# Output products of an attention kernel as two row-tiled products of 64 channels, added when they are evicted

## The chip, the cores and the metric

The kernel runs on one core of a Trainium2 chip. The metric is the device time of the whole kernel in microseconds (us). A core has TensorE (matrix products, written to PSUM), VectorE, ScalarE (activations, evictions), GpSimd and SyncE (which here only issues DMA transfers). In the profile they are called PE, DVE, ACT, POOL and SP; PEld is TensorE's loading of weights, which overlaps its products. [...]

## The reference

Two layers of attention over images of 32 x 32 positions with 768 channels, four images, all fp32. Both have the same form; the second has biases on its projections and a scale that is applied twice. Cut to what matters:

```python
for layer in (0, 1):
    h = group_norm(x)                                  # 32 groups of 24 channels
    q, k, v = split(h @ Wqkv)                          # 12 heads of 64 channels
    bias = rel_h(q)[..., :, None] + rel_w(q)[..., None, :]
    attn = softmax(scale * q @ k.T + bias)             # 1024 x 1024 per head
    x = x + (attn @ v) @ Wproj + bproj
```

## The kernel before, in words

Everything is channel-major: a tile has channels on its 128 partitions and positions along its free axis. An image and layer count as one "image", `im` 0 to 7 (layer 0's four, then layer 1's four). The twelve heads go in six pairs of two heads, `pair` 0 to 5, and a pair's 1024 queries in eight blocks of 128, `n` 0 to 7. A unit is one (pair, n). The main loop runs over all 8 x 6 x 8 units in an order written out by hand; every engine takes its instructions in the order in which the loop issues them.

In each unit:

- `biases` adds the two relative-position terms on GpSimd for the unit two ahead (L319).
- `scores` for the next unit: products q k on TensorE (tile `s`, L333; a head has 64 channels, so the products of two heads are row-tiled: each uses one half of the array's rows). Two passes on VectorE take the sum with the bias and its extreme (L342, shown as CUSTOM_DVE), ScalarE takes the exponential.
- `turn` transposes the unit's weights in blocks of 32 x 32 on VectorE (tile `tb`, L370). After every second unit the tile is written to DRAM (`td`, L373) and read back in another layout (`pt`, L381). A quarter of the queries is two units. All these transfers are issued by SyncE.
- `divide` takes a reciprocal on VectorE (L353) behind the transposes, and GpSimd multiplies the next unit's weights by it (L356).
- A share of a list `todo` of other products fills TensorE: the projections of the next pair (`pj` L214, `pv` L249, 36 steps), then output products (`o` L475, 12 steps). In most pairs these shares are 6, 6, 0, 6, 12, 6, 0, 12 steps in units 0 to 7, so all of a pair's output products, four groups of three, fall into unit 7. In that unit `first` is 3: one group comes in front of the transposes, three behind them.
- At n = 6 `weigh` multiplies v with the transposed weights of quarters 0 and 1 (tile `av`, L399; column-tiled by 64), at n = 2 of the next pair those of quarters 2 and 3.

An output group takes 128 output channels by 512 positions and half of the input channels (part `p` 0 in pairs 3 to 5, part 1 in pairs 0 to 2 of the next image; the last image has three parts). It is three products of 128 channels into one PSUM bank. VectorE then adds it to what was there: to the residual and the bias (`scalar_tensor_tensor`, L486) for part 0, to the partial sum (`tensor_tensor`, L488) for part 1. For layer 0's part 1 statistics of the sum follow (L152, L154). The result is stored by SyncE (L493), issued at the start of the next unit, ahead of the read back of quarter 3.

In pair 4 the next image's six chunks are normalised on VectorE (`apply`, L193): chunks 0 to 2 in earlier units, 3 to 5 in unit 7 between the groups. `pj` of the next unit reads them.

PSUM tiles of TensorE's products other than `s` come from one pool `ps_m` with two buffers of two banks; `s` has two such tiles of its own. `pj` and `pv` are already in the form that the change gives to `o`: two row-tiled products of 64 channels into two banks, the first evicted by ScalarE and the second added by VectorE. In the last image there is no next pair; its last pair (and its tail) is filled with output products alone, whose weights `wo` are fetched by SyncE four groups ahead.

Of the kernel before, what the change touches and what calls it, by code (L numbers as in the profile page):

```python
# [31 lines left out]
FP = mybir.dt.float32  # L32
AF = mybir.ActivationFunctionType
ALU = mybir.AluOpType
ENGINES = {getattr(mybir.EngineType, e) for e in ("PE", "DVE", "Activation", "Pool", "SP")}

P = 128
B, HW, C = 4, 32, 768
S = HW * HW
NH, D = 12, 64  # L40
NC = C // P
NT = S // P
# [3 lines left out]
HALF = 512  # L46
LAYERS = 2
NP = NH // 2
# [6 lines left out]
def attention_blocks(ctx: ExitStack, tc: tile.TileContext, a: dict, out: bass.AP):  # L55
    nc = tc.nc
# [19 lines left out]
    ps_m = ctx.enter_context(tc.tile_pool(name="ps_m", bufs=2, space=PSUM))  # L76
# [9 lines left out]
    xn_of, w_of, wo_of = {im: [] for im in range(NI)}, {}, {}  # L86
# [31 lines left out]
    for l in range(LAYERS):  # L118
        tab = const.tile([P, 2, 2 * HW], FP, tag=f"tab{l}", name=f"tab{l}")
        nc.gpsimd.memset(tab, 0.0)  # L120
        for i, ax in enumerate("hw"):
            src = a[f"rel{ax}{l}"]
            n = src.shape[1]
# [9 lines left out]
    bo = []  # L133
    for l in range(LAYERS):
        t = const.tile([P, NC], FP, tag=f"bo{l}", name=f"bo{l}")
# [11 lines left out]
    def stats(im, c, i, x):  # L147

        if i == 0:
            half_stats[im] = small.tile([P, 2, 6], FP, tag="st", name=f"st_{im}_{c}")  # L150
        st = half_stats[im]
        nc.vector.bn_stats(st[:, i, :], x)  # L152
        if i == 1:
            nc.vector.bn_aggr(mv_of[im][:, c, :], st.rearrange("p i s -> p (i s)"))  # L154
# [155 lines left out]
    sc_of, st_of, tb_of, pt_of, attn_of = {}, {}, {}, {}, {}  # L310
# [40 lines left out]
    def divide(g, n):  # L351
        st = st_of[g, n]
        nc.vector.reciprocal(st[:, 2, :], st[:, 1, :])  # L353
        for h in range(2):
            sc = sc_of[g, n, h].rearrange("p k j -> p (k j)")
            nc.gpsimd.tensor_scalar(sc, sc, st[:, 2, h : h + 1], 1.0, ALU.mult, ALU.mult)  # L356
# [59 lines left out]
    def cuts(im):  # L416
        return [0, NC // 2, NC] if im + 1 < NI else [0, NC // 2, NC - 1, NC]
# [49 lines left out]
    def project_out(im, p, o, i):  # L467
        l, b = images[im]
        end = im + 1 == NI
        rows = slice(o * P, (o + 1) * P)  # L470
        cols = slice(i * HALF, (i + 1) * HALF)
        c0, c1 = cuts(im)[p : p + 2]
        t = ps_m.tile([P, S], FP, tag="m", name=f"o_{im}_{p}_{o}_{i}")[:, :HALF]
        for c in range(c0, c1):
            nc.tensor.matmul(  # L475
                t, lhsT=wo_of[im, o, c], rhs=attn_of[im * NP + c][:, cols],
                start=(c == c0), stop=(c == c1 - 1),
            )
            if c < c1 - 1:
                yield True  # L480
        if end and (p, i) == (0, 0):
            sum_of[o] = xpool.tile([P, S], FP, tag="xn", name=f"sum_{o}")
        to = sum_of[o][:, cols] if end else res_of[im, p, o, i]
        if p == 0:
            res = res_of[im, p, o, i]
            nc.vector.scalar_tensor_tensor(to, t, bo[l][:, o : o + 1], res, ALU.add, ALU.add)  # L486
        else:
            nc.vector.tensor_tensor(to, t, to, ALU.add)  # L488
        if p == 1 and l + 1 < LAYERS:
            stats(im + B, o, i, to)  # L490
        dst = (part_of[im] if p == 0 and not end else dsts[l][b])[rows, cols]
        if not end:
            early.append(lambda: nc.sync.dma_start(out=dst, in_=to))  # L493
        elif p == 2:
            nc.sync.dma_start(out=dst, in_=to)
        if i == 1 and (im, p, o, i) in place:
            if end:
                fetch(place[im, p, o, i] + 4)
            else:
                later.append(lambda: fetch(place[im, p, o, i] + 4))  # L500
        yield True
# [7 lines left out]
    def run(todo):  # L509
        while todo:  # L510
            todo.pop(0)()

    def prepare(g):

        todo = [(project_in(g, which, i), NC) for which in range(2) for i in range(2) if g < NPAIR]
        if g % 2:
            return todo + [(project_values(g - 1, i), NC) for i in (2, 3)]
        return todo + [(project_values(g, i), NC) for i in (0, 1) if g < NPAIR]
# [5 lines left out]
    def take(groups, n):  # L524

        while groups and n > 0:
            group, count = groups[0]
            if next(group, None) is None:
                groups.pop(0)
            else:  # L530
                groups[0] = (group, count - 1)
                n -= 1
        while groups and groups[0][1] == 0:
            for _ in groups.pop(0)[0]:
                pass
# [6 lines left out]
    with tc.manual_schedule(engines=ENGINES):  # L542
        for c in range(NC):
            for i in range(2):
                stats(0, c, i, xn_of[0][c][:, i * HALF : (i + 1) * HALF])
        stages, apply = norm(0)
        for n in sorted(stages):
            stages[n]()
        for c in range(NC):
            apply(c)  # L550
        todo = prepare(0)
        take(todo, 2 * NC)
        mid.pop(0)()
        take(todo, NC)
        mid.pop(0)()
        later.pop()()
        take(todo, 2 * NC)
        run(later)
        fetch(3)
        biases(0, 0)  # L560
        scores(0, 0)
        divide(0, 0)
        biases(0, 1)

        units = [(g, n) for g in range(NPAIR) for n in range(NT)]
        for at, (g, n) in enumerate(units):
            im, pair = divmod(g, NP)
            end = im + 1 == NI
            if n == 0:
                shares = [6, 6, 0, 6, 12, 6, 0, 12]  # L570
                ins = (todo if at == 0 else []) + prepare(g + 1)
                if pair < 3:
                    if at == 0:
                        shares = [12, 6, 0, 6, 12, 6, 0, 0]
                    todo = ins + (put_out(im - 1, 1, range(4 * pair, 4 * pair + 4)) if im else [])
                elif pair < NP - 1:
                    todo = ins + put_out(im, 0, range(4 * pair - 12, 4 * pair - 8))
                    if pair == 3 and not end:
                        stages, apply = norm(im + 1)
                else:  # L580
                    todo = ins + put_out(im, 0, range(8, 12))
                    if end:
                        fetch_last()
                        todo += put_out(im, 1, range(12)) + put_out(im, 2, range(0, 12, 2))
                        shares = [6, 6, 0, 6, 6, 2, 0, 4]
            if (pair, n) in loads and not end:
                load_x(im + 1, loads[pair, n])
            if im + 1 < B:
                if (pair, n) in loads0:
                    load_x(im + 1, loads0[pair, n], loads0[pair, n] + AHEAD)  # L590
                if pair < 3 and n in (1, 3, 5, 6):
                    c, i = divmod(4 * pair + n // 2, 2)
                    x = xn_of[im + 1][c % AHEAD][:, i * HALF : (i + 1) * HALF]
                    later.append(lambda c=c, i=i, x=x: stats(im + 1, (c + AHEAD) % NC, i, x))
            run(early)
            early, later = later, early
            if at + 2 < len(units):
                biases(*units[at + 2])
            if at + 1 < len(units):
                scores(*units[at + 1])  # L600
            run(behind)
            behind, behind2 = behind2, behind
            if pair == 3 and n in stages and not end:
                stages[n]()
            if pair == 4 and n in (2, 4, 6) and not end:
                apply(n // 2 - 1)
            share = shares[n]
            first = 3 if n == NT - 1 else 2 if end and pair == NP - 1 and n in (3, 4) else 0
            first = min(first, share)
            take(todo, first)  # L610
            share -= first
            turn(g, n)
            if at + 1 < len(units):
                divide(*units[at + 1])
            if pair == 4 and n == 7 and not end:
                for chunks in ((3, 4), (5,)):
                    take(todo, 3)
                    share -= 3
                    for c in chunks:
                        apply(c)  # L620
            take(todo, share)
            if n == 6:
                weigh(g, (0, 1))
            elif n == 2 and g:
                weigh(g - 1, (2, 3))
        for read in behind:
            read(nc.scalar)
        take(todo, 12)
        for quarter in (2, 3):
            weigh(NPAIR - 1, (quarter,))  # L630
        todo = put_out(NI - 1, 2, range(1, 12, 2))
        take(todo, len(todo))
# [55 lines left out]
```

## Time and profile before

| | |
|---|---|
| time, median of 3 | 3507.43 us (3504.42 to 3509.01) |
| profiled span | 3507.0 us |
| granted TensorE clock | 0.998 |
| busy: PE, DVE, ACT, POOL | 99%, 68%, 35%, 78% |
| output products (o), instructions and busy time | 1080 + 72, 475.8 + 33.5 us |
| eviction of part 0, mean of one (L486) | 743 ns, 84 of them, and 12 of the last image |
| eviction of part 1, mean of one (L488) | 680 ns, 84 of them, and 24 of the last image |
| 32 x 32 transposes, mean of one (L370) | 1222 ns, 768 of them |
| DMA, mean over the span | 309 GB/s |

Busy time of TensorE is taken from modelled ends of pipelined products, and overlapping instructions of one group are counted once. An fp32 product appears as two instructions, so three products are six. The chain of waits is the better view of what a product costs: it lists pieces by their starts, and a piece lasts until the next begins.

### The profile page before, as it was taken

How to read it: one execution, taken by the hardware profiler on the slowest of the kernel's cores; microseconds unless marked ns; L12 is line 12 of the kernel's file. 1: busy time of each engine (PE TensorE's matmuls, PEld its weight loads, DVE VectorE, ACT ScalarE, POOL GpSimd, SP SyncE). 2: the span in 40 equal slices, each digit the busy share in tenths (PEclk: the TensorE clock that was granted, in tenths of full speed). 3: DMA queues.
4: the chain of work that ended last, by engine and by line, in shares of the span. 5: the costliest groups of instructions: out<-in, count | busy, mean ns of one | idle time of the engine just before them, and what ended most of it. 6: DMA issues, size and time to landing. Idle time of an engine off the chain costs nothing.

```text
span 3507.0 us, 55102 instructions
## 1 busy us (share of the span) xinstructions
PE 3462.3 (99%) x21120; PEld 1921.4 (55%) x21120; DVE 2381.1 (68%) x3676; ACT 1227.5 (35%) x2040; POOL 2729.9 (78%) x1546
## 2 busy tenths in 40 slices
PE   6999999999999999999999999999999999999999
PEld 4555555555555555555555555555555555555554
DVE  4666767767677676767767667666666667666666
ACT  2334333333333333333333333333333333333331
POOL 3888887778777787788777788787787778787774
PEclk9999999999999999999999999999999999999999
DMA  4889989999899898898989989899889988898877
GB/s 137 312 308 311 332 293 337 319 316 326 304 329 323 313 316 313 312 324 305 326 305 326 320 292 332 311 331 306 300 327 324 321 298 316 319 322 295 311 275 281
DMA packets 624857, 1084.54 MB, mean 309 GB/s; under 512 B 247120, under 2 KB 310096, under 8 KB 575440
## 3 DMA queue, kind: packets, MB, share of 16 engines
q1 hardware_dynamic: 569008, 1028.29, 83.4%
q10 hardware_dynamic: 55584, 52.72, 4.4%
q8 instruction: 166, 2.72, 0.3%
q14 instruction: 99, 0.81, 0.1%
HBM read 580.59 MB, written 500.27 MB: 308 GB/s over the span
## 4 chain that ended last, share of the span: by engine, by line
PE 97%; DMA 2%; DVE 0%; SPq 0%; issue 0%; ACT 0%; POOL 0%; ACTq 0%; DVEq 0%
PE pj L214 28%; PE s L333 19%; PE av L399 19%; PE o L475 14%; PE pv L249 14%; PE tp L281 3%; DMA tdr<-t 1%; DMA pt<-td 1%; SPq L307 0%; DMA td<-tb 0%; DMA wo<-in_wo 0%; DMA xn<-in_x 0%; DVE st L152 0%; DMA rel<-tdr 0%; DMA per<-mv 0%
## 5 line engine op out<-in xcount | busy, mean ns | idle before, releaser
L319 POOL TENSOR_TENSOR sc<-rel 128x1024 f32<-128x1024 f32 x768 | 1890.4, 2485 | 38.2 <-DMA rel<-tdr 38.2
L356 POOL TENSOR_SCALAR sc<-sc,sm 128x1024 f32<-128x1024 f32 x768 | 855.1, 1127 | 686.1 <-DVE sm L353 669.2
L346 ACT ACTIVATE sc<-sc,sm 128x1024 f32<-128x1024 f32 x768 | 879.8, 1147 | 1370.9 <-DVE sm L342 1368.7
L342 DVE CUSTOM_DVE_ANT_0 sc<-s,sc 128x1024 f32<-128x1024 f32 x768 | 909.8, 1222 | 293.3 <-PE s L333 266.4
L214 PE MATMUL pj<-xn,w 64*128 64x512 f32 x4608 | 1033.5, 591 | 26.8 <-DVE xn L193 25.7
L370 DVE STREAM_TRANSPOSE tb<-sc 128x1024 f32<-128x1024 f32 x768 | 910.7, 1222 | 22.9 <-DMA td<-tb 20.5
L214 PEld LDWEIGHTS pj<-xn,w 64*128 64x128 f32 x4608 | 453.2, 188 | 568.6 <-issue 536.6
L333 PE MATMUL s<-k,q 64*128 64x512 f32 x3072 | 750.1, 598 | 7.0 <-DVE sm L342 6.9
L399 PE MATMUL av<-pt,v 128*64 128x256 f32 x6144 | 689.1, 382 | 6.1 <-DMA pt<-td 6.1
L399 PEld LDWEIGHTS av<-pt,v 128*64 128x64 f32 x6144 | 434.5, 137 | 289.8 <-ACT v L259 35.6
L249 PE MATMUL pv<-wv,xn 64*128 64x256 f32 x4608 | 515.7, 376 | 0.0
L249 PEld LDWEIGHTS pv<-wv,xn 64*128 64x128 f32 x4608 | 448.3, 187 | 90.8 <-issue 30.1
L475 PE MATMUL o<-attn,wo 128*128 128x512 f32 x1080 | 475.8, 597 | 0.2 <-DMA wo<-in_wo 0.2
L333 PEld LDWEIGHTS s<-k,q 64*128 64x128 f32 x3072 | 288.5, 187 | 299.5 <-issue 275.5
L475 PEld LDWEIGHTS o<-attn,wo 128*128 128x128 f32 x1080 | 201.4, 190 | 271.4 <-issue 260.9
L260 DVE TENSOR_TENSOR v<-pv,v 128x256 f32<-128x256 f32 x192 | 81.5, 425 | 277.6 <-ACT v L259 277.6
L259 ACT COPY v<-pv 128x256 f32<-128x256 f32 x192 | 71.5, 372 | 330.7 <-PE pv L249 282.9
L286 ACT COPY t<-tp 128x1024 f32<-128x1024 f32 x96 | 97.2, 1012 | 245.5 <-PE tp L281 148.5
L346 ACT ACTIVATION_READ_ACCUMULATOR sc<-sc,sm 128x1 f32 x768 | 143.6, 187 | 0.0
L230 DVE TENSOR_TENSOR q<-pj,q 128x512 f32<-128x512 f32 x96 | 66.4, 692 | 107.5 <-ACT q L227 56.0
L230 DVE TENSOR_TENSOR k<-pj,k 128x512 f32<-128x512 f32 x96 | 66.4, 692 | 95.5 <-ACT k L227 49.0
L281 PEld LDWEIGHTS tp<-tab,q 64*128 64x128 f32 x1536 | 100.0, 187 | 39.9 <-issue 39.6
(34 smaller groups left out, 787.6 us busy)
## 6 DMA issues: line engine op xcount, KB each, us to landing
td<-tb SPq DMA_DIRECT2D x384, 1024.0 KB, 5.9
pt<-td SPq DMA_DIRECT2D x382, 1024.0 KB, 7.6
tdr<-t ACTq DMA_DIRECT2D x96, 512.0 KB, 6.3
w<-in_wqk SPq DMA_DIRECT2D x96, 384.0 KB, 7.5
rel<-tdr SPq DMA_DIRECT2D x760, 32.0 KB, 2.3
part<-res SPq DMA_DIRECT2D x84, 256.0 KB, 5.5
res<-part SPq DMA_DIRECT2D x84, 256.0 KB, 9.1
wv<-in_wv SPq DMA_DIRECT2D x24, 768.0 KB, 8.7
```

The source lines that it names most:

```text
L214: nc.tensor.matmul(t[:, a, :], lhsT=w[rows, c, :], rhs=xn[c][rows, cols], start=(c == 0), stop=(c == NC - 1),)
L230: nc.vector.tensor_tensor(to, t[1], to, ALU.add)
L249: nc.tensor.matmul(t[:, a, k, :], lhsT=xn[c][rows, (2 * i + k) * P : (2 * i + k + 1) * P], rhs=w[rows, c, :], start=(c == 0), stop=(c == N ...
L281: nc.tensor.matmul(ps[:, h, j, :], lhsT=q[rows, at * P : (at + 1) * P], rhs=tabs[l][rows, :], start=True, stop=True,)
L319: nc.gpsimd.tensor_tensor(sc.rearrange("p (a k) (u l) -> p a (k u) l", a=4, l=8), rel[:, h, 0, n, :].unsqueeze(1).unsqueeze(3).to_broadcas ...
L333: nc.tensor.matmul(ps[h][:, cols], lhsT=q[rows, n * P : (n + 1) * P], rhs=k[rows, cols], start=True, stop=True,)
L342: nc.vector.tensor_tensor_reduce(out=sc, in0=ps[h], in1=sc, scale=-scale, scalar=BIG, op0=ALU.add, op1=ALU.min, accum_out=st[:, 0, h : h + 1],
L346: nc.scalar.activation(sc, sc, AF.Exp, bias=st[:, 0, h : h + 1], scale=-1.0, accum_out=st[:, 1, h : h + 1],)
L356: nc.gpsimd.tensor_scalar(sc, sc, st[:, 2, h : h + 1], 1.0, ALU.mult, ALU.mult)
L370: nc.vector.transpose(tb[:, :, j, :], sc_of[g, n, h])
L399: nc.tensor.matmul(av[rows, at * 2 * P : (at + 1) * 2 * P], lhsT=v_of[g][:, k, rows], rhs=pt_of[g, quarter, h][:, :, k, :], start=(k == 0) ...
L475: nc.tensor.matmul(t, lhsT=wo_of[im, o, c], rhs=attn_of[im * NP + c][:, cols], start=(c == c0), stop=(c == c1 - 1),)
```

## The change

Each output product over 128 channels becomes two over 64, one for each half of the array's rows, into the two banks of the same tile. The eviction then has two steps on VectorE: the old one on the first bank, and a new `tensor_tensor` that adds the second. It is for keeping TensorE in one tiling: the products in front and behind are row-tiled by 64.

In unit 7 two groups (`first` 6 steps) are now taken in front of the transposes instead of one. In pair 4 the order behind the transposes was group, chunks 3 and 4, group, chunk 5, group; it is now group, chunks 3 and 4, group, chunk 5.

```diff
-        t = ps_m.tile([P, S], FP, tag="m", name=f"o_{im}_{p}_{o}_{i}")[:, :HALF]
+        t = ps_m.tile([P, 2, HALF], FP, tag="m", name=f"o_{im}_{p}_{o}_{i}")
         for c in range(c0, c1):
-            nc.tensor.matmul(
-                t, lhsT=wo_of[im, o, c], rhs=attn_of[im * NP + c][:, cols],
-                start=(c == c0), stop=(c == c1 - 1),
-            )
+            for h in range(2):
+                of = slice(h * D, (h + 1) * D)
+                nc.tensor.matmul(
+                    t[:, h, :], lhsT=wo_of[im, o, c][of, :], rhs=attn_of[im * NP + c][of, cols],
+                    start=(c == c0), stop=(c == c1 - 1),
+                )
...
-            nc.vector.scalar_tensor_tensor(to, t, bo[l][:, o : o + 1], res, ALU.add, ALU.add)
+            nc.vector.scalar_tensor_tensor(to, t[:, 0, :], bo[l][:, o : o + 1], res, ALU.add, ALU.add)
         else:
-            nc.vector.tensor_tensor(to, t, to, ALU.add)
+            nc.vector.tensor_tensor(to, t[:, 0, :], to, ALU.add)
+        nc.vector.tensor_tensor(to, t[:, 1, :], to, ALU.add)
...
-            first = 3 if n == NT - 1 else 2 if end and pair == NP - 1 and n in (3, 4) else 0
+            first = 6 if n == NT - 1 else 2 if end and pair == NP - 1 and n in (3, 4) else 0
...
             if pair == 4 and n == 7 and not end:
-                for chunks in ((3, 4), (5,)):
-                    take(todo, 3)
-                    share -= 3
-                    for c in chunks:
-                        apply(c)
+                take(todo, 3)
+                share -= 3
+                for c in (3, 4):
+                    apply(c)
             take(todo, share)
+            if pair == 4 and n == 7 and not end:
+                apply(5)
```

## Prediction

> **What bounds the kernel now.** I read the page's busy shares first, then the chain that ended last, then that chain cut to one period.
>
> ```profile
> PE 3462.3 (99%) x21120; PEld 1921.4 (55%) x21120; DVE 2381.1 (68%) x3676; ACT 1227.5 (35%) x2040; POOL 2729.9 (78%) x1546
> ...
> PE 97%; DMA 2%; DVE 0%; SPq 0%; issue 0%; ACT 0%; POOL 0%; ACTq 0%; DVEq 0%
> ```
>
> TensorE is never idle and 97% of the chain is its own. What counts is what a product costs on TensorE, and whether another engine gets late enough to stop it. The chain around one run of output products, in order of time (start us, us, what):
>
> ```profile
> 1039.83 1.92 PE s L333 x8
> 1041.75 10.50 PE o L475 x24
> 1052.25 1.92 PE s L333 x8
> 1054.16 5.15 PE pj L214 x24
> 1059.31 1.72 PE s L333 x8
> ...
> 1066.18 0.89 PE tp L281 x16
> ...
> 1068.79 7.06 PE av L399 x64
> 1075.85 1.09 PE tp L281 x16
> ```
>
> Each product is two instructions. Read two things. A pair of 64-channel products of 512 columns costs 5.15 / 6 = 0.858 us (pj, 24 instructions = 6 pairs), so 12 pairs would be 10.30; 12 products of 128 channels cost 10.50. Row tiling in itself brings nothing: the whole difference is 0.20 us, once per run. And s takes 1.72 between pieces in its own tiling, 1.92 after o or av; tp takes 0.89, and 1.09 after av. So each change of tiling costs 0.20 us, booked on the piece behind it. A run of o has two of them, s to o and o to s. The same 10.50 piece recurs every 71.7 us, 43 times from 324.80 to 3335.99, and once more in part from 3407.68.
>
> **What the Trainium skill says.** "TensorEngine Tiling (Array Packing)", Key Properties: changing the tiling mode drains TensorE. The trace agrees: 0.20 us. Same page, PSUM Bottleneck: tiling speeds up TensorE but not the emptying of PSUM, and row tiles write to different banks. Here it doubles the emptying: two bank-sized reads for one. "SBUF — State Buffer", Who interferes with whom: a VectorE tensor_scalar can hold the port pair shared with GpSimd, while an instruction with one SBUF input outside such a mode does not contend. The trace agrees on the first: the normalisation (xn, L193) takes 1.20 us alone and 2.27 beside the bias sum on GpSimd. The added sum has one PSUM and one SBUF input, so I give it no such penalty.
>
> **The change part by part.**
>
> Row tiling: 44 full runs lose two switches, 44 x 0.40 = 17.6 us; the two first runs of the last pair give some 0.8 more. About -18 us, all on the chain, as nothing else is. PSUM tiles were two banks before (half of one unused), so the rotation of two buffers is unchanged.
>
> Second sum per group: 192 more VectorE instructions (180 + 12 groups), 0.69 us each by the row `res<-o,res`. An eviction is then about 1.42 us (0.78 from a dependent start to the next, 0.64 to an independent one), 1.36 where the first is itself a TENSOR_TENSOR. VectorE gains 130 us of work at 68% busy. In the middle this is hidden by its idle time unless it delays something with a deadline.
>
> Two groups in front of the transposes: this is that delay. Counted from the start of o, now: group 1 is evicted at 2.8, transposes 3.5 to 5.8. After: group 1 evicted 2.61 to 4.03, VectorE waits for group 2 (2 x 2.575 = 5.15), evicts it to 6.6 (7.5 where statistics of the sum are taken as well, which is in pairs 0 to 2 of images 1 to 4), transposes 6.6 to 8.9 (7.5 to 9.8). So td is issued 3.05 (3.25) us later. Behind it in SyncE's queue stand the stores of res and then the read back pt, which av (quarters 2 and 3) needs at 27.04 now, 26.65 after. The queue of a run with statistics (the timeline of SyncE, start us and us; each line holds x issues):
>
> ```profile
> 616.98 1.46 SPq L373 DMA_DIRECT2D td<-tb  x2
> 618.49 1.20 SPq L94 DMA_DIRECT2D xn<-in_x  x1
> 619.74 5.01 SPq L493 DMA_DIRECT2D mid<-res  x4
> 624.85 1.71 SPq L381 DMA_DIRECT2D pt<-td  x2
> ```
>
> and its two reads in the list of DMA issues of that stretch (the last number is the median us from issue to landing):
>
> ```profile
> pt<-td SPq DMA_DIRECT2D x2, 1024.0 KB, 9.7
> ```
>
> There is no gap between these issues, and the DMA engines are 90% busy, so a later td moves all of it. The run starts at 611.58; the two reads start at 13.3 and 14.3 and land at 22.3 and 24.9: 2.2 us to spare. I took start and landing of the second read in all 44 runs. Spare time is 2.2 to 3.9 in the runs of pairs 0 and 1 of images 1 to 6, 2.8 to 5.8 at pair 5, 3.9 to 6.6 nearly everywhere else. Needed is 3.25 + 0.40 = 3.65 (3.45 without statistics). Shortfalls: four runs of pair 0, 0.7 to 1.1 each; three of pair 1 0.4 to 1.5; a few of 0.1 to 0.7: 8 us together. If the transfers close up, 0; if landings scatter more, 14. I take 7.
>
> Pair 4, n = 7, where three chunks of the next image are normalised on VectorE in the same unit (the timeline of VectorE, start us and us, from the second eviction on):
>
> ```profile
> 833.11 2.73 DVE L193 TENSOR_SCALAR xn<-xn,nrm 128x1024 f32<-128x1024 f32 x2
> 835.76 0.73 DVE L486 SCALAR_TENSOR_TENSOR res<-o,bo,res 128x512 f32<-128x512 f32 x1
> 836.42 2.27 DVE L193 TENSOR_SCALAR xn<-xn,nrm 128x1024 f32<-128x1024 f32 x1
> 838.60 0.74 DVE L486 SCALAR_TENSOR_TENSOR res<-o,bo,res 128x512 f32<-128x512 f32 x1
> 839.26 1.21 DVE L342 CUSTOM_DVE_ANT_0 sc<-s,sc 128x1024 f32<-128x1024 f32 x1
> ```
>
> VectorE has no gap here as it is; the score pass (L342) comes at 12.6 from the start of o (826.66). After: transposes end 8.9, group 3 to 10.4, two normalisations 2.65 (up to 3.5, as they now meet the bias sum on GpSimd), group 4 1.42, the third 2.2: 16.6 to 17.4. Two scores have to leave PSUM before s of the next unit, which TensorE reaches at 17.2: they leave at 18.9 to 19.7, and the last chunk is ready 0.3 to 1.3 after pj wants it. TensorE loses 1.5 to 2.3, less if the port clash is milder; I take 1.8 in seven runs, 13 us. In the other pairs the score pass comes by 14.2 at the latest, its PSUM is free at 16.4: no stop.
>
> Last pair. wo of its groups is loaded behind td in SyncE's queue and already ends a wait:
>
> ```profile
> 3413.97 6.21 DMA wo<-in_wo
> ```
>
> It lands at 12.5 from the start of o (3407.68), after the change 3.05 later at 15.6, where o could start at 12.0: +3 net. Then units of three short groups need 2.3 + 2.3 + 3 x 1.36 = 8.7 us of VectorE against 6.9 of TensorE: +2.2 over n = 3 to 5 with the buffers' slack. At n = 7 two groups instead of one stand before the last transposes: one more product pair of two (1.72) and its longer eviction, +2.4 on the path td, pt, av. The six last groups run at 1.36 of VectorE instead of 0.86: 9.2 instead of 6.5, +2.7. Tail +7.
>
> Moving normalisation of chunk 5 behind the last group: counted above. GpSimd's divide waits for the reciprocal behind the transposes and comes 3 us later; it idled 3.0 to 3.7 us there, so nobody waits.
>
> Sum: -18 + 7 + 13 + 3 + 7 = +12, less a little since two late things in one run overlap: +10.6. 3507.4 + 10.6 = 3518.
>
> **Rivals.** (a) The late transposes are absorbed: reads land just in time and pair 4 loses 0.8 us a run: -18 + 6 + 3 + 7 = -2, 3505, no change. For it: no av in the middle waits now; against: 2 us of spare time in places and an unbroken queue. (b) TensorE alone decides: -18 and at most the tail's 7, so 3489 to 3497, faster. For it: 97% of the chain; against: three places with less slack than the shift of 3. (c) The delay spreads, with av late by 1 us in half the runs: +12 and 10 more, 3530; DMA at 90% speaks for it, the recovery within each 71 us period against it.
>
> **How the numbers follow.** Likeliest the forecast, with (c) on its side: 0.60 (0.50 and 0.10). (a) 0.26, (b) 0.14. The bound of 0.2% is 7 us, 3500.4 to 3514.4: faster is (b), same is (a). The range leaves out most of (b) and the far end of (c): 3499 to 3530.
>
> **What would show it.** Right: o in 10.30 and s behind it in 1.72; transposes 3 us later in the run; VectorE's score pass, or xn, ending waits of s or pj at pair 4; av waiting for pt in pairs 0 and 1; the last six groups paced by VectorE. Wrong: a period of 71.3 us throughout, with no wait of av or s between 330 and 3400; or o pieces other than 10.30.

## The result and the profile after

The changed kernel takes 3595.49 us (3594.89 to 3608.32) beside 3506.48 for the kernel before: ratio 1.0262, 95% interval 1.0238 to 1.0286. It is slower by some 89 us, more than eight times the 10.6 that were forecast, and outside the range. The profiled execution is the longest of them, with a span of 3606.5 us.

The page after, busy shares and the chain by engine:

```profile
PE 3492.3 (97%) x22272; PEld 1952.4 (54%) x22272; DVE 2524.9 (70%) x3880; ACT 1221.3 (34%) x2040; POOL 2727.6 (76%) x1546
...
PE 71%; DMA 18%; DVE 4%; SPq 4%; issue 1%; POOL 1%; ACT 1%; ACTq 0%; DVEq 0%; POOLq 0%
```

TensorE has fallen from 97% of the chain to 71%; transfers and the queue that issues them carry most of the rest. What TensorE waited for (us in total, times, longest):

```profile
PE av L399 <- DMA pt<-td: 54.5, 26, 3.9
PE pj L214 <- DVE xn L193: 34.6, 8, 25.6
```

The first was 6.1 us in 3 waits before, the second 25.7 in one (the start). The chain of waits around one run of output products (start us, us, what):

```profile
606.36 4.82 PE pv L249 x45
611.18 8.70 DMA pt<-td
619.87 0.04 issue
619.92 3.67 PE av L399 x30
623.58 1.92 PE s L333 x8
625.50 10.30 PE o L477 x48
635.80 1.72 PE s L333 x8
```

Both halves can be seen here. o takes 10.30 instead of 10.50 and the s behind it 1.72 instead of 1.92: the saving of 0.40 us a run is there to the digit. But an av stopped in its middle for a transposed tile. The chain lists that transfer at its whole length from issue to landing. TensorE worked through most of it and then stood idle for 2.63 us, as its own timeline says:

```profile
619.92 3.67 PE L399 MATMUL av<-pt,v 128*64 128x256 f32 x30 [2.63 <-DMA pt<-td]
```

From the first run of o to the 43rd it was 3335.99 - 324.80 = 3011.2 us. Now it is 3432.82 - 326.67 = 3106.2. Forty-two periods of 71.295 would be 2994.4, so 16.8 us are won and 111.8 lost. Seven periods that contain pair 4's unit 7 take 74.3 (one of them 75.8), which is 22.3 us of the loss. The other 89.5 are in nineteen periods of 72.4 to 79.2. In all of these av waits for pt at n = 6, 66 to 71 us from the start of o, and in none of them at n = 2, where the wait was forecast. From the 43rd run to the end it is 173.7 us instead of 171.0.

Not all of the 89.5 us is waiting. The waits that the trace lists for TensorE in the nineteen periods add up to some 56. Another part is the granted clock. Between the first run of o and the 43rd it is at half in eleven stretches, ten of 3.4 us and one of 6.8; in the kernel before it is never at half there. Ten of the stretches lie at the restart of an av that had stood idle for 2.5 us or more, the eleventh behind the wait in the period of 75.8. Here is the second part of such an av in the chain, and then the busy times of PE, PEld, DVE, ACT and POOL over the stretch, followed by the clock (0.50), the DMA share and GB/s:

```profile
990.83 5.35 PE av L399 x30
990.90:994.30 3.40, 3.40 (x18) 1.89 (x20) 0.90 (x1) 0.00 (x0) 0.00 (x0) 0.50 1.01 426
```

Thirty such instructions take 5.35 us here and 3.67 above. Half of the 41 us at half clock, some 20, is an estimate of what this costs, 19 of it in the nineteen periods. That the stops bring the lower clock isn't tested by itself; the run below in which av doesn't stop has one such stretch between the same two runs of o. The remaining 15 us of the 89.5 aren't put down to anything here.

**Where the 89 us are lost.** The timeline of SyncE in the kernel before, in the period whose o starts at 539.88 (start us, us; x issues):

```profile
562.87 1.60 SPq L373 DMA_DIRECT2D td<-tb  x2
...
570.55 3.44 SPq L381 DMA_DIRECT2D pt<-td  x2
580.50 1.46 SPq L373 DMA_DIRECT2D td<-tb  x2
582.00 1.19 SPq L94 DMA_DIRECT2D xn<-in_x  x1
583.36 11.84 SPq L307 DMA_DIRECT2D rel<-tdr  x16
595.29 0.95 SPq L381 DMA_DIRECT2D pt<-td  x2
```

and after, in the period whose o starts at 550.46:

```profile
575.43 3.03 SPq L373 DMA_DIRECT2D td<-tb  x2
...
585.19 3.00 SPq L381 DMA_DIRECT2D pt<-td  x2
590.68 1.46 SPq L373 DMA_DIRECT2D td<-tb  x2
592.18 1.32 SPq L94 DMA_DIRECT2D xn<-in_x  x1
602.86 7.73 SPq L307 DMA_DIRECT2D rel<-tdr  x16
610.68 0.95 SPq L381 DMA_DIRECT2D pt<-td  x2
```

The relative-position terms of the next pair take a way of their own. TensorE's products tp (L281) are copied by ScalarE into a tile t, in two halves, and each half is written to DRAM (tdr, issued by ScalarE). Sixteen small reads (rel, L307, issued by SyncE) bring them back in the layout that `biases` needs. ScalarE's timeline has the two writes that rel waits for, before and after:

```profile
566.30 0.37 ACTq L288 DMA_DIRECT2D tdr<-t  x1
576.56 1.02 ACT L286 COPY t<-tp 128x1024 f32<-128x1024 f32 x1 [5.85 <-DMA tdr<-t]
577.61 0.37 ACTq L288 DMA_DIRECT2D tdr<-t  x1
```

```profile
579.36 0.37 ACTq L288 DMA_DIRECT2D tdr<-t  x1
590.08 1.01 ACT L286 COPY t<-tp 128x1024 f32<-128x1024 f32 x1 [7.93 <-DMA tdr<-t]
591.12 0.37 ACTq L288 DMA_DIRECT2D tdr<-t  x1
```

Read relative to the start of o, the delay goes round as follows. Transposes start at 7.7 instead of 4.2, about as forecast, so td of quarter 3 and its read back are late, and the loads of wo and res behind them. The two td writes of quarter 0 (units 0 and 1 of the next pair) are issued at 25.0 and 27.8 instead of 23.0 and some 24.4. VectorE waits for one of their buffers in unit 2:

```profile
585.24 1.25 DVE L370 STREAM_TRANSPOSE tb<-sc 128x1024 f32<-128x1024 f32 x1 [4.47 <-DMA td<-tb]
```

The first tdr of ScalarE goes out at 28.9 from the start of o instead of 26.4: its tile was copied by 576.44, but it was issued at 579.36, 0.08 us after the landing of a load of res (579.28; why it waits for that is in the last section). It lands at 39.5 instead of 36.6. There is one buffer for t, so the second copy waits for the landing, and the second tdr is issued at 591.12, behind the td of quarter 1 (590.68). Before, it was issued at 577.61, three microseconds in front of that td (580.50). The list of DMA issues in short windows around the two gives its time to landing, before:

```profile
tdr<-t ACTq DMA_DIRECT2D x1, 512.0 KB, 4.4
```

and after:

```profile
tdr<-t ACTq DMA_DIRECT2D x1, 512.0 KB, 11.7
```

Two or three microseconds of delay have turned an order round, and this transfer takes seven longer. It is so in the whole trace: the second tdr takes 9.4 to 12.8 us in eighteen of the nineteen periods that lose time at av (4.8 in the nineteenth, which loses 1.1), and 4.2 to 6.8 in the other twenty-three. In the kernel before it takes 4.1 to 6.4 in all forty-two. The sixteen small reads of rel wait for it at the head of SyncE's queue: nothing is issued between 592.18 + 1.32 and 602.86. The read back of quarter 1 stands behind them, issued at 60.2 from the start of o instead of 55.4. It is wanted in the middle of av at n = 6, behind quarter 0's 3.5 us: that is the stop in front of 619.92, as the second of its two transfers was issued at 611.18 and landed at 619.87. In the whole trace, SyncE's rel issues waited 229.4 us for tdr, 52.3 before.

**Pair 4.** VectorE in unit 7, o starting at 847.13:

```profile
853.72 2.36 DVE L370 STREAM_TRANSPOSE tb<-sc 128x1024 f32<-128x1024 f32 x2
...
857.42 4.39 DVE L193 TENSOR_SCALAR xn<-xn,nrm 128x1024 f32<-128x1024 f32 x2
861.73 0.74 DVE L488 SCALAR_TENSOR_TENSOR res<-o,bo,res 128x512 f32<-128x512 f32 x1
...
863.12 1.54 DVE L193 TENSOR_SCALAR xn<-xn,nrm 128x1024 f32<-128x1024 f32 x1
864.58 1.21 DVE L342 CUSTOM_DVE_ANT_0 sc<-s,sc 128x1024 f32<-128x1024 f32 x1
```

and TensorE beside it:

```profile
864.71 1.13 PE L214 MATMUL pj<-xn,w 64*128 64x512 f32 x4 [1.28 <-DVE xn L193]
865.85 2.70 PE L333 MATMUL s<-k,q 64*128 64x512 f32 x7
```

The score pass comes 17.4 us from the start of o (forecast 16.6 to 17.4), pj has to wait for the third chunk and s for the score pass: 3.0 us a period.

### The profile page after: what moved, and what is told of

Its sections match the earlier page's. It is cut to its first block, busy times and chain, and to the rows that moved or that the text cites. A ratio compares the mean times of both kernels' runs of the same rounds, so it can differ in the third digit from the quotient of the medians.

```text
span 3606.5 us, 57605 instructions
## 1 busy us (share of the span) xinstructions
PE 3492.3 (97%) x22272; PEld 1952.4 (54%) x22272; DVE 2524.9 (70%) x3880; ACT 1221.3 (34%) x2040; POOL 2727.6 (76%) x1546
## 4 chain that ended last, share of the span: by engine, by line
PE 71%; DMA 18%; DVE 4%; SPq 4%; issue 1%; POOL 1%; ACT 1%; ACTq 0%; DVEq 0%; POOLq 0%
PE pj L214 20%; PE av L399 14%; PE s L333 14%; PE o L477 12%; PE pv L249 9%; DMA tdr<-t 8%; DMA pt<-td 6%; SPq L307 3%; DMA res<-part 2%; PE tp L281 2%; DMA wo<-in_wo 1%; DVE xn L193 1%; DVE tb L370 1%; DMA td<-tb 1%; POOL sc L319 0%
## 5 line engine op out<-in xcount | busy, mean ns | idle before, releaser
L370 DVE STREAM_TRANSPOSE tb<-sc 128x1024 f32<-128x1024 f32 x768 | 914.1, 1222 | 204.4 <-DMA td<-tb 204.2
L399 PE MATMUL av<-pt,v 128*64 128x256 f32 x6144 | 717.8, 389 | 54.7 <-DMA pt<-td 54.5
L399 PEld LDWEIGHTS av<-pt,v 128*64 128x64 f32 x6144 | 444.2, 140 | 357.6 <-DMA pt<-td 67.2
L477 PE MATMUL o<-attn,wo 64*128 64x512 f32 x2160 | 471.2, 589 | 0.0
L333 PEld LDWEIGHTS s<-k,q 64*128 64x128 f32 x3072 | 297.8, 188 | 294.1 <-issue 254.3
L477 PEld LDWEIGHTS o<-attn,wo 64*128 64x128 f32 x2160 | 209.2, 187 | 254.3 <-issue 253.9
L286 ACT COPY t<-tp 128x1024 f32<-128x1024 f32 x96 | 97.2, 1013 | 333.6 <-DMA tdr<-t 267.9
L281 PEld LDWEIGHTS tp<-tab,q 64*128 64x128 f32 x1536 | 104.2, 187 | 38.5 <-issue 37.9
L491 DVE TENSOR_TENSOR res<-o,res 128x512 f32<-128x512 f32 x168 | 116.2, 692 | 5.8
```

Source lines behind the costliest of these rows:

```text
L281: nc.tensor.matmul(ps[:, h, j, :], lhsT=q[rows, at * P : (at + 1) * P], rhs=tabs[l][rows, :], start=True, stop=True,)
L333: nc.tensor.matmul(ps[h][:, cols], lhsT=q[rows, n * P : (n + 1) * P], rhs=k[rows, cols], start=True, stop=True,)
L370: nc.vector.transpose(tb[:, :, j, :], sc_of[g, n, h])
L399: nc.tensor.matmul(av[rows, at * 2 * P : (at + 1) * 2 * P], lhsT=v_of[g][:, k, rows], rhs=pt_of[g, quarter, h][:, :, k, :], start=(k == 0) ...
L477: nc.tensor.matmul(t[:, h, :], lhsT=wo_of[im, o, c][of, :], rhs=attn_of[im * NP + c][of, cols], start=(c == c0), stop=(c == c1 - 1),)
L491: nc.vector.tensor_tensor(to, t[:, 1, :], to, ALU.add)
```

## The experiments

Times are medians, ratios are to the kernel before on the same chip.

**One group in front of the transposes again.** Row tiling stays.

```diff
-            first = 6 if n == NT - 1 else ...
+            first = 3 if n == NT - 1 else ...
...
-                take(todo, 3)
-                share -= 3
-                for c in (3, 4):
-                    apply(c)
+                for chunks in ((3, 4), (5,)):
+                    take(todo, 3)
+                    share -= 3
+                    for c in chunks:
+                        apply(c)
```

> Row tiling and the second sum stay; one group in front of the transposes and the old order in pair 4. Theory L (the late transposes push td, the read backs and the relative-position reads behind each other in the DMA queue): transposes start at about 4.0 us (4.7 with statistics) instead of 6.8 and 7.7, av's waits for pt nearly vanish, 3485 to 3505 us. Rival V (the doubled eviction overloads VectorE wherever it stands): 3560 to 3600, waits of av for pt stay above 30 us. Rival P (row-tiled o is itself the trouble on TensorE): 3560 to 3600 with no waits.

Measured: 3529.41 us, ratio 1.0065 (1.0052 to 1.0078). Two thirds and more of the loss are gone and av waits 3.5 us for pt in the whole trace. But L had it at 3485 to 3505, below the kernel before, and it isn't: a miss. TensorE's waits show why:

```profile
PE pj L214 <- DVE xn L193: 26.3, 1, 26.3
PE o L477 <- DVE res L491: 8.9, 12, 0.9
PE pj L214 <- DVE res L491: 8.0, 7, 1.1
```

Group 2 is now evicted behind the transposes, with two sums, and the two PSUM buffers are full when group 4 wants to start: the period is 71.7 (72.3 where statistics follow, 73.1 in pair 4) instead of 71.3. So moving two groups in front cured something. The price of the cure is the late transposes. V and P fall, with a rest for V: two sums do need a place.

**The order alone.** The kernel before with `first = 6` and the new order in pair 4, and nothing else.

```diff
-            first = 3 if n == NT - 1 else ...
+            first = 6 if n == NT - 1 else ...
```

> The old products of 128 channels and single evictions, but two groups in front of the transposes. Theory L: transposes start at about 6.1 us (6.8 with statistics), 2.6 later than before instead of 3.2, so the same waits in a smaller number: 3540 to 3590 us, av's waits for pt 20 to 50 us. Rivals V and P: 3505 to 3512, no waits.

Measured: 3541.50 us, ratio 1.0093 (1.0079 to 1.0107), the low end of what L said. TensorE's first two waits:

```profile
PE pj L214 <- DVE xn L193: 25.7, 1, 25.7
PE av L399 <- DMA pt<-td: 25.3, 15, 3.9
```

The old products, the old evictions, and the same wait of av. Late transposes (6.1 and 7.0 us) are enough for a loss of 34 us, without row tiling and the second sum. These make the transposes later still (6.8 and 7.7), and pair 4's loss is theirs (no wait for xn here but the one at the start).

**The loads of wo and res moved out of the way.** The changed kernel, with the fetch issued in unit 4.

```diff
-                later.append(lambda: fetch(place[im, p, o, i] + 4))
+                fetches.append(lambda: fetch(place[im, p, o, i] + 4))
...
             behind, behind2 = behind2, behind
+            if n == 4:
+                run(fetches)
```

> The changed kernel, with the loads of the next wo and res moved from the start of unit 0 to unit 4, where they aren't queued in front of td of units 0 and 1. Theory L: the transposes stay late (6.8 and 7.7 us), but td of quarter 0 lands some 3 us earlier and VectorE no longer waits for the buffer at unit 2; av's waits for pt fall below 15 us and the time to 3510 to 3535 (pair 4 still loses 3 us in seven runs). Rivals V and P: 3580 to 3600.

Measured: 3522.87 us, ratio 1.0042 (1.0026 to 1.0057). Transposes are as late as before the move, but av waits 4.6 us for pt instead of 54.5, and rel waits 48.8 us for tdr instead of 229.4. What is left is pair 4's 3 us, and in four runs a wait for res, which now comes late itself. VectorE still waits 127.0 us for td (204.2 in the changed kernel), more than L allowed for. Whether it is the bytes of these six transfers that count or only their places in the queue isn't told apart here.

**Both together.**

```diff
-            first = 6 if n == NT - 1 else ...
+            first = 3 if n == NT - 1 else ...
...
-                later.append(lambda: fetch(place[im, p, o, i] + 4))
+                fetches.append(lambda: fetch(place[im, p, o, i] + 4))
```

> Both: one group in front of the transposes, and the loads moved to unit 4. Theory L: no more than the first of these runs gains, 3480 to 3500 us, as nothing is late there. Rivals: as for the first run.

Measured: 3538.29 us, ratio 1.0089 (1.0075 to 1.0103), some 9 us above the first run: a miss. There is no late td to cure, and the late loads of res hold up evictions in seven periods, which take up to 74.3.

**Only the queue's order.** The changed kernel with the small rel reads issued behind the read back of quarter 1.

```diff
-            later.append(lambda: diagonals(g))
+            (rels if g else later).append(lambda: diagonals(g))
...
             behind, behind2 = behind2, behind
+            if n == 4:
+                run(rels)
```

> The changed kernel, with one thing moved: the sixteen small reads of the relative positions (rel from tdr) are issued in unit 4 behind the read back of quarter 1 instead of in unit 3 in front of it. Transposes stay at 6.8 and 7.7 us. Theory L2 (the lost time comes from SyncE's queue: the small reads wait there for a late tdr, and the read back of quarter 1 stands behind them): av's waits for pt fall from 54 us to below 15, the time to 3515 to 3545 us (pair 4 still loses 3 us in seven runs), while VectorE goes on waiting about 200 us for td. Rival D (the DMA engines are simply behind by the delay): av's waits stay above 35 us, 3575 to 3600.

Measured: 3516.07 us, ratio 1.0023 (1.0014 to 1.0032). This is the run that settles the cause: transposes, products, evictions and bytes are those of the changed kernel, and 79 of the 89 us are gone. SyncE's timeline in a period whose o starts at 538.8:

```profile
579.22 1.46 SPq L373 DMA_DIRECT2D td<-tb  x2
580.73 1.26 SPq L94 DMA_DIRECT2D xn<-in_x  x1
585.57 3.29 SPq L381 DMA_DIRECT2D pt<-td  x2
591.31 9.72 SPq L307 DMA_DIRECT2D rel<-tdr  x16
```

The read back of quarter 1 goes out 46.8 us from the start of o (60.2 in the changed kernel), and av doesn't wait for pt at all. ScalarE goes on waiting for tdr as long as before the move (256.2 us, 267.9 in the changed kernel): the transfer is still late, but nothing that TensorE needs stands behind it. VectorE's wait for td fell to 107.6 us; I had expected it to stay near 200, so about half of it went with the held queue. Rival D falls.

The control is the kernel before with the same move:

> The kernel before, with the small relative-position reads issued behind the read back of quarter 1. Theory L2: that order is worth something only where tdr is late; before, nothing waits for it in the middle, so 3504 to 3511 us, the same. Rival (the move is good for any kernel here, and says nothing about the late transposes): 3470 to 3495.

Measured: 3502.87 us, ratio 0.9983 (0.9977 to 0.9990). It gains 5 us, not nothing: just below what L2 allowed (3504), and well short of the rival (3495 or less). The periods of its trace stay at 71.7, and what is gained lies before the first run of o and after the 43rd. At most some 5 of the 79 us can be what the move is worth by itself.

**One group in front of each transpose.**

```diff
-            take(todo, first)
-            share -= first
-            turn(g, n)
+            for h in range(2):
+                take(todo, min(3, share))
+                share -= min(3, share)
+                turn(g, n, (h,))
```

> Row tiling and second sum everywhere, but in unit 7 one group is evicted in front of each of the two transposes, statistics come behind both, and in pair 4 chunks 3 and 4, group, chunk 5, group. Transposes at about 4.1 and 6.6 us, PSUM of group 2 free at 6.6, before group 4 wants it at 7.7. If the losses are where the transposes and evictions stand, the period is 71.3 us with some 0.5 lost in pair 4 and 3491 to 3503 us; if the second sum costs by itself wherever it is, 3520 or more, as with one group in front.

Measured: 3501.15 us, ratio 0.9982 (0.9975 to 0.9989). The first transpose starts at 4.1 to 4.2 us (3.5, or 4.2 with statistics, before the change), and group 2's buffer is free in time. The period is 71.3, and 72.2 in pair 4, but for one of 76.4 in which av waits for pt at n = 6 again.

**The end untiled.** On top of it, parts 1 and 2 of the last image as whole products with one sum.

```diff
+        whole = end and p > 0
...
-        nc.vector.tensor_tensor(to, t[:, 1, :], to, ALU.add)
+        if not whole:
+            nc.vector.tensor_tensor(to, t[:, 1, :], to, ALU.add)
```

> The same, and the groups of parts 1 and 2 of the last image as products of 128 channels with one sum, since nothing else is on TensorE there and VectorE sets the pace. If the tail is paced by the second sum, 4 to 6 us below the run before: 3486 to 3499. Otherwise within 2 us of it.

Measured: 3496.35 us, ratio 0.9970 (0.9959 to 0.9982), 4.8 below the run before, within what was expected of a tail paced by VectorE.

**All of it.** The last kernel with the rel reads moved too.

> The last kernel with one group in front of each transpose and untiled products at the end, and the small reads behind the read back of quarter 1. Theory L2: little is late there, so within 3 us of 3496; if single executions still lose some us to a late tdr, this takes that away and the spread shrinks, 3490 to 3496.

Measured: 3489.83 us, ratio 0.9946 (0.9932 to 0.9960), the fastest here, 0.5% below the kernel before. It gains 6.5 us on the run before and is just outside what was expected; the spread did not shrink (7.4 us in five executions, 5.1 in seven of the run before). In its trace the 42 periods are the same, 71.3 each, and 72.2 in pair 4; the first run of o starts 6 us earlier. What is won lies in the first image, where no output products fill unit 7.

## Why the prediction was wrong

- **Row tiling, -18 us: right.** o takes 10.30, the s behind it 1.72, and 16.8 us are won over 42 periods. In the run with all changes the period is the forecast 71.3.
- **Transposes 3.05 to 3.25 us later: right.** They start at 6.76 and 7.67 us from the start of o, 3.2 and 3.45 later than before (6.6 and 7.5 were forecast).
- **Late reads of quarter 3, +7 us: wrong, and no loss at all.** I took the read back of quarter 3 to be wanted at the start of av in unit 2. av takes quarter 2 first, whose 3.5 us stand in front of it. In the period shown, the later read of quarter 3 lands 27.6 us from the start of o; av starts at 26.7 and doesn't stop, as it reaches quarter 3 at 30.3.
- **The step that failed** is the sentence on rival (c), that "the recovery within each 71 us period" speaks against a spreading delay, and with it the 3 us taken as a shift that ends at quarter 3. I followed the late td to its first reader and stopped. The delay went on through the loads behind that td, the next td and the first tdr, the single t buffer and a changed order of tdr and td, and came out of SyncE's queue at quarter 1, some 60 us after the transposes: 89.5 us, where +7 was put for all late reads and rival (c) allowed 10 more. There was a sign of it in the profile before: ScalarE waited there for tdr 15 times, 89.4 us in all, and rel and pt share one queue. The forecast counted who waits for td, not who waits for what is queued behind td's neighbours.
- **Pair 4, +13 us: the mechanism right, the size off.** It cost 22.3, some 3.0 a run where I took 1.8, and 1.5 more in the run beside a stretch of half clock. The term that was too small is the normalisation of chunks 3 and 4: 4.31 us for both, where I took 2.65 and allowed 3.5. The third was shorter than taken, 1.46. The score pass came at the top of the forecast range, for which I had allowed 2.3; pj's wait (1.3) and what s then still lacks add up to more.
- **Last pair, wo +3 us: wrong.** In the last image the fetch is called by a group with i = 1. With two groups in front of the transposes that call stands in front of td, so wo was issued earlier than before, not later (5.2 us from the start of o, 6.3 before): o of the next unit begins without a wait.
- **Tail, +7 us: too large.** From the 43rd run to the end the kernel lost 2.7 us, after the 0.4 of that run's own saving. The last six groups are paced by VectorE as forecast. Untiling the end gives back 4.8 us.
- **GpSimd's divide: right,** it idled longer, and VectorE's waits for it are 4.9 us in all (7.9 before).
- **The count of second sums, 192: wrong, without effect.** It takes the 1152 instructions of o as 192 groups of six, but a group of the last image has only four (two products). There are 204 groups, and the page has 204 more VectorE instructions; VectorE gained 144 us instead of 130.

The sum was +12 for -18 and 30 of losses; it became some +89 for about -18 and 107, and four fifths of the loss is the one term that was not in it. What the Trainium skill says in "TensorEngine Tiling (Array Packing)", Key Properties, of the drain holds at 0.20 us. In "SBUF — State Buffer", Who interferes with whom, a VectorE instruction in a two-port mode that meets the shared ports while GpSimd has them blocks entirely: chunks 3 and 4 at 2.2 us each, beside 1.20 alone, fit that, but no run here takes GpSimd away from them.

## What to carry to other kernels

When a change delays the issue of a transfer, follow it past its first reader: through every buffer that the transfer frees, through what the same issuing queue holds behind it, and up to the same point of the next period. Here a queue that issues in order made of some 3 us of lateness 9.4 us in which nothing was issued, so put transfers that wait for a far producer behind those that TensorE needs soon. And where an eviction is doubled, place it between pieces of the work that has the deadline, not in front of all of it.

## What the runs showed that I had not expected

- In the two periods shown, a transfer of 512 KB issued 3 us in front of 2 MB of others lands in 4.4 us; issued half a microsecond behind the first of them it lands in 11.7.
- td of quarter 0 was not issued when its transpose ended but 0.06 us after the read back of quarter 3, which had landed after 8.17 us in the chain. In the trace both hold the same semaphore; the transfers take eight of them in turn, and four issues of that stretch (two of td, one of w, the first tdr) come 0.06 to 0.08 us after the landing of the eighth issue before them. So a late transfer also delays later ones that don't touch its data.
- Moving sixteen small reads by one unit is worth 79 us in one kernel, 6.5 in another and 5 in a third, with the same bytes in all.
